# Opening of a gated attention-and-experts layer: first weight loaded by tile, the norm's root ahead of the weight's absolutes, all weight products on GpSimd, second weight's maxima beside the first's

## The chip, the cores and the metric

The kernel runs on one core of one Trainium2 chip. A core has a matrix engine (TensorE, in the profile PE for its products and PEld for its weight loads), a vector engine (VectorE, DVE), a scalar engine (ScalarE, ACT), a general engine (GpSimd, POOL) and a sync engine (SyncE, SP) that here issues most of the loads and stores. Each engine works through its own list of instructions in order, and waits on semaphores for the others. The metric is the device time of one execution in microseconds.

## What is computed

The input is `x`, four batches of 512 tokens with 512 features. Two layers follow, each with a residual. The first is a SmoothQuant pair of int8 linears with a gated unit between them, with the weights `fside` (512 x 512, in the kernel `wi`) and `ctx` (512 x 256, `wc`), one of each per batch. The second is a mixture of sixteen experts, top two per token, beside a shared expert.

```python
def _smooth_quant_linear(x, w):
    amax_x = jnp.max(jnp.abs(x), axis=0)
    amax_w = jnp.max(jnp.abs(w), axis=0)
    s = jnp.sqrt(jnp.maximum(amax_x, EPS) / jnp.maximum(amax_w, EPS))
    xs = x / s
    ws = w * s
    x_scale = jnp.maximum(jnp.max(jnp.abs(xs), axis=-1, keepdims=True), EPS) / QMAX
    w_scale = jnp.maximum(jnp.max(jnp.abs(ws), axis=-1, keepdims=True), EPS) / QMAX
    x_q, w_q = round_and_clip(xs / x_scale), round_and_clip(ws / w_scale)
    return x_q @ w_q.T * x_scale * w_scale.T

x = x + tanh(g_xattn) * down(silu(gate) * up)      # both by _smooth_quant_linear of layernorm(x)
x = x + tanh(g_ffn) * (experts(layernorm(x)) + shared(layernorm(x)))
```

(`round_and_clip` and the last two lines are shortened here.) What matters below is the order that the formula forces on one linear: the column maxima of `|x|` and of `|w|` must both be known before `s` is; `s` before the products `x / s` and `w * s`; these before their row maxima; and the row maxima before anything can be rounded and multiplied.

## The kernel before

A tile is 128 rows. A batch of `x` is four tiles of 128x512, `wi` is four tiles of 128x512, `wc` four of 128x256. Batches go one after the other through both linears; the shared expert's products on TensorE (float32, 128x512) are there to fill TensorE beside them. After all four batches come the sixteen experts, and at the end the results are gathered and added.

Three parts of the code set the order. The stretch from the second half of batch 0 on is laid out by a planner (`Plan`) that knows estimated durations. Before it, for batch 0 and the start of batch 1, the order is written by hand: `opening.at(time, steps)` puts steps on a list, sorted by the time given and then by their place in the text. The times only sort; nothing waits for them. The list is then run once, and so gives each engine its instructions in that order.

The steps that the change touches, with the lines of the kernel before:

- `load_tokens(b)` and `load_weights(b)` (lines 166 to 175) issue the loads of a batch on SP: four tiles of `x`, then `wi` as one transfer of 1 MB, then `wc` as one of 512 KB. Lines 177 to 179 do this for batches 0 and 1, and after them come the two gates (`tg_x_raw`, `tg_f_raw`), the router's weight `gate_sb` and the shared expert's weights. The loads use eight semaphores in turn, so that SP holds the ninth load back until the first has landed, and so on.
- `f0` is the first linear of batch 0. `f0.stats` are mean and variance of a tile (DVE L289, L290). `f0.norm` has three steps: the variance plus epsilon (DVE L272), its root on ACT (L263), and on DVE a reciprocal and a Newton step that end in `r` and `nmr` (L276 to L283). `f0.abs_max` takes `|x|` of a normed tile on ACT (L448) and folds it into the column maximum on DVE (L452).
- `wide0` are the column maxima of `wi`, `narrow0` those of `wc`: `absolute(t)` takes `|w|` of a tile on ACT (L410), `greater(t)` folds it in on DVE (L414), `turn` transposes the maximum on TensorE (L296), `end` reduces it and takes a reciprocal on DVE (L421 to L423). The absolutes of tile 0 have a buffer of their own (`amw`), the others share three (`ab`) with those of `x`.
- `f0.turn_max` and `f0.column_max` do the same for `x` (L296, L464). `f0.smooth` has three steps: the quotient under the root (DVE L313), its root on ACT (L263), and on DVE a Newton step and reciprocals (L318 to L322).
- `f0.row_rs` and `f0.row_s` spread `1/s` and `s` over all partitions (TensorE L304); the second is copied to SBUF by ACT (L475, `s_row`).
- `f0.divide(t)` makes `xn` (DVE L485), `f0.multiply(t)` makes `wi * s` on POOL or DVE (L490). `f0.max_x` and `f0.max_w` are the row maxima, each one reduction over four tiles on DVE (L328), `scale_x` and `scale_w` the small steps behind them (L334 to L339).
- `steps_x`, `steps_w` round to int16 (ACT L348, DVE L346), `turn_x_tile` and `turn_w_tile` transpose on TensorE (L358), `take_x` and `take_w` copy out of PSUM (L351), `product(t)` multiplies (TensorE L565), `scale(t)` writes `h` (DVE L573), and silu, `times_up` and the column maxima of the gated result follow (L576, L583, L587, L590).
- `s0` is the second linear of batch 0, with steps of the same names; its `multiply(t)` is L637, and its `max_w` is again L328.
- `f1.stats(t)`, the statistics of batch 1, are put in between, where they are thought to fit.

PSUM tiles come from three pools: `ps_t` (two buffers), `ps_c` (two) and `ps_mm` (four). `chain_ps` in the code stands for the first two, `beside_ps` for the third.

Of the kernel before, what the change touches and what calls it, by code (L numbers as in the profile page):

```python
# [14 lines left out]
AF = mybir.ActivationFunctionType  # L15
# [105 lines left out]
def flamingo_gated_kernel(  # L121
# [44 lines left out]
    def load_tokens(b):  # L166
        for t in range(TT):
            nc.sync.dma_start(out=X[:, b * TT + t, :], in_=x_flat[:, b * TT + t, :])

    def load_weights(b):  # L170
        wi = qa.tile([P, HC, H], F32, tag="wi", name="wi", bufs=2)
        nc.sync.dma_start(out=wi, in_=w_in[b].rearrange("(t p) d -> p t d", p=P))
        wc = qb.tile([P, HC, A], F32, tag="wc", name="wc", bufs=2)
        nc.sync.dma_start(out=wc, in_=w_ctx[b].rearrange("(t p) d -> p t d", p=P))
        W[b].wi, W[b].wc = wi, wc

    for b in range(2):
# [79 lines left out]
    def small(n, name):  # L257
        return stat.tile([P, n], F32, tag=name, name=name)
# [67 lines left out]
    def row_max(t3, h):  # L326
        sc = small(TT, "sc" + h)
        vec.tensor_reduce(sc, t3, axis=AX.X, op=ALU.max, apply_absolute_value=True)  # L328
        return sc
# [68 lines left out]
    def weights(b, ps=chain_ps):  # L398
        w = W[b]
        w.raw = {}  # L400

        def part(w3, n, h):
            v = SimpleNamespace()

            v.ab = {}
# [6 lines left out]
            def greater(t):  # L412
                v.am = v.ab[0]
                vec.tensor_tensor(v.am[:, :n], v.am[:, :n], v.ab[t][:, :n], ALU.max)  # L414

            def turn():
                v.tp = columns(ps, v.am, n // P)

# [4 lines left out]
                vec.reciprocal(raw, raw)  # L423
                w.raw[n // P] = raw

            return SimpleNamespace(absolute=absolute, greater=greater, turn=turn, end=end)

        return part(lambda: w.wi, H, "i"), part(lambda: w.wc, A, "c")


    def first(b):
# [102 lines left out]
        def sent_w():  # L534
            steps_to_float(w.wqT)

        def max_w():
            w.ws = row_max(w.wi, "w1")

        def scale_w():  # L540
            v.rws = row_scales(w.ws, "w1")
# [63 lines left out]
    def second(b):  # L605
# [75 lines left out]
        def sent_w():  # L681
            steps_to_float(v.wqT)

        def max_w():
            v.ws = row_max(w.wc, "w2")

        def scale_w():
            v.rws = row_scales(v.ws, "w2")
# [563 lines left out]
    opening.at(27.0, *each(f0.steps_x), *each(f0.turn_x_tile))  # L1252
    opening.at(30.0, lambda: f0.steps_w(3), *each(f0.steps_w, vec, ts=[0, 1, 2]))
    opening.at(30.5, *each(f0.turn_w_tile, ts=[0, 1, 3, 2]), lambda: f0.take_x(0, vec), lambda: f0.take_x(2, act))
    opening.at(32.0, lambda: f0.take_w(0, vec), lambda: f0.take_w(2, act), f0.row_ws, *each(narrow0.absolute), *each(narrow0.greater, ts=[1, 2, 3]))
    opening.at(33.6, lambda: f0.product(0), lambda: f0.scaled(0), lambda: f0.product(1), lambda: f0.times_up(0))
    opening.at(35.0, narrow0.turn, lambda: f0.scaled(1), lambda: f0.times_up(1), lambda: f0.gated_abs(0), narrow0.end)
    opening.at(36.0, lambda: f0.product(2), lambda: f0.scaled(2), lambda: f0.times_up(2), lambda: f0.gated_abs(1))
    opening.at(37.0, lambda: f0.product(3), lambda: f0.scaled(3), lambda: f0.gated_greater(1))
    opening.at(38.7, lambda: f0.times_up(3, vec), lambda: f0.gated_max(2), lambda: f0.gated_max(3))  # L1260
# [487 lines left out]
```

## Time and profile before

| what | value |
|---|---|
| median of 3 runs | 585.71 us (585.59 to 585.83) |
| the profiled execution, its own time | 585.57 us |
| its span, first to last instruction | 583.5 us |
| PE busy in the span | 529.3 us, 91% |
| DVE busy | 405.1 us, 69% |
| ACT busy | 228.9 us, 39% |
| POOL busy | 138.2 us, 24% |
| DMA, mean | 163 GB/s |

The span is 2.1 us shorter than the execution's time; these lie outside the first and last instruction. The busy tenths of the page's forty slices (14.6 us each) show where PE isn't full:

```profile
PE   0375499999999999999989999999999999999994
```

Every digit but the first five and the last is 8 or 9. The opening, which the change rewrites, is in these first five slices.

A line of the timeline, as used below, has the start of a group of instructions in us from the span's start, how long the group took, the engine, the line of the kernel, the operation, what it writes and reads, its shape and how many instructions the group has; in brackets stands idle time of the engine before it and what ended it.

### The profile page before, as it was taken

To read this page: it belongs to the slowest core of one execution; us is meant where nothing else is said; L and a number is where in the kernel's file an instruction comes from. 1 tells how busy PE (TensorE), PEld (TensorE's weight loads), DVE (VectorE), ACT (ScalarE), POOL (GpSimd) and SP (SyncE) were. 2 spreads that over 40 slices of the span, in tenths; PEclk is the share of its full clock that TensorE was granted. 3 is DMA by queue.
4 is the path that set the end of the run, shared out by engine and by line. 5 is a ranking of instruction groups with operands and counts; after the bars stand their busy time and mean duration, and the time that the engine had idled before them with its cause. 6 is when DMAs were issued, how large, how long until landed. Compare 5 with 4: busy or idle time off the path is not lost.

```text
span 583.5 us, 5816 instructions
## 1 busy us (share of the span) xinstructions
PE 529.3 (91%) x1760; PEld 275.0 (47%) x1764; DVE 405.1 (69%) x926; ACT 228.9 (39%) x380; POOL 138.2 (24%) x152
## 2 busy tenths in 40 slices
PE   0375499999999999999989999999999999999994
PEld 0232345444444444454455555555555555544441
DVE  3878778998999898987278666666666666304474
ACT  3465366646824272050135434434435343211000
POOL 1212130344143421100310111111212110007770
PEclk9995699999999999999999999999999999999999
DMA  8971012011402365010587999999999995215695
GB/s 295 359 229 38 0 54 92 0 38 54 91 1 54 56 232 155 20 72 1 131 209 223 264 249 269 276 236 276 262 260 274 276 276 173 87 72 160 200 319 187
DMA packets 93774, 95.05 MB, mean 163 GB/s; under 512 B 51488, under 2 KB 69920, under 8 KB 93744
## 3 DMA queue, kind: packets, MB, share of 16 engines
q1 hardware_dynamic: 84016, 69.52, 44.5%
q0 software_dynamic: 5120, 16.78, 9.2%
q10 hardware_dynamic: 4608, 8.39, 3.8%
q8 instruction: 14, 0.23, 0.2%
q14 instruction: 16, 0.13, 0.1%
HBM read 66.36 MB, written 16.78 MB: 142 GB/s over the span
## 4 chain that ended last, share of the span: by engine, by line
PE 79%; DVE 4%; issue 2%; POOL 1%; ACT 0%; DVEq 0%; POOLq 0%
PE b L1138 22%; PE eo L974 14%; PE pu L959 11%; PE pg L959 11%; PE sh L1024 9%; PE pr L998 2%; PE tp_h L1158 2%; PE acc L565 2%; PE sh L1030 1%; PE rowb L304 1%; PE acc L713 1%; DVE amw_w L414 1%; PE tp_am L296 1%; PE tp_x L760 1%; PE tp_q L358 1%
## 5 line engine op out<-in xcount | busy, mean ns | idle before, releaser
L974 PE MATMUL eo<-wd,ehT 128*128 128x512 f32 (+1 forms) x192 | 85.1, 592 | 0.0
L1089 POOL DMA_INDIRECT xg<-xn_dram,slot_token x32 | 34.8, 1088 | 195.7 <-DMA xp<-xg 161.0
L959 PE MATMUL pg<-xT,wsg 128*128 128x512 f32 x160 | 75.7, 603 | 0.0
L959 PE MATMUL pu<-xT,wsu 128*128 128x512 f32 x160 | 74.0, 595 | 0.0
L1024 PE MATMUL sh<-wsd,hT 128*128 128x512 f32 x160 | 73.9, 597 | 0.0
L974 PEld LDWEIGHTS eo<-wd,ehT 128*128 128x128 f32 (+1 forms) x192 | 36.4, 190 | 42.1 <-issue 37.7
L351 ACT COPY xgT<-xp 128x1024 int16<-128x1024 int16 x31 | 39.5, 1339 | 26.4 <-DMA xp<-xg 26.3
L1187 DVE TENSOR_TENSOR p<-p,b 128x352 f32<-128x352 f32 x16 | 8.3, 521 | 58.8 <-PE b L1138 58.8
L1659 POOL DMA_INDIRECT yk<-eo_dram,slot x32 | 33.5, 1048 | 55.7 <-PE pu L959 46.3
L959 PEld LDWEIGHTS pu<-xT,wsu 128*128 128x128 f32 x160 | 29.3, 190 | 31.2 <-issue 31.1
L1024 PEld LDWEIGHTS sh<-wsd,hT 128*128 128x128 f32 x160 | 28.9, 190 | 31.4 <-issue 30.4
L959 PEld LDWEIGHTS pg<-xT,wsg 128*128 128x128 f32 x160 | 29.0, 193 | 30.3 <-issue 29.5
L1138 PE MATMUL b<-T,S 128*128 128x352 f32 x128 | 40.6, 460 | 0.7 <-DVE S L1129 0.7
L1138 PE MATMUL b<-wg,xgT 128*128 128x352 f32 x128 | 40.6, 460 | 0.0
L1138 PE MATMUL b<-wu,S 128*128 128x352 f32 x128 | 40.5, 459 | 0.0
L1149 ACT COPY eo_sb<-eo 128x512 f32<-128x512 f32 x32 | 18.7, 585 | 47.5 <-PE eo L974 43.5
L1138 PEld LDWEIGHTS b<-T,S 128*128 128x128 f32 x128 | 24.2, 190 | 14.5 <-issue 1.2
L1138 PEld LDWEIGHTS b<-wu,S 128*128 128x128 f32 x128 | 24.3, 190 | 13.5
L490 POOL TENSOR_TENSOR wi<-wi,s_row 128x512 f32<-128x512 f32 x15 | 18.6, 1274 | 46.8 <-ACT s_row L475 46.8
L966 DVE TENSOR_TENSOR hT<-g,pu 128x512 f32<-128x512 f32 x20 | 13.6, 682 | 22.6 <-PE pu L959 22.2
L963 ACT ACTIVATE g<-pg 128x512 f32<-128x512 f32 x20 | 11.9, 596 | 41.9 <-PE pg L959 35.6
L1670 DVE SCALAR_TENSOR_TENSOR X<-yk,wk,X 128x512 f32<-128x512 f32 x32 | 23.1, 748 | 7.4 <-DMA yk<-eo_dram,slot 7.1
(219 smaller groups left out, 857.5 us busy)
## 6 DMA issues: line engine op xcount, KB each, us to landing
wg<-in_L_ffn_w_gate_dram SPq DMA_DIRECT2D x16, 704.0 KB, 5.0
wu<-in_L_ffn_w_up_dram SPq DMA_DIRECT2D x16, 704.0 KB, 6.2
wd<-in_L_ffn_w_down_dram SPq DMA_DIRECT2D x16, 512.0 KB, 5.8
eo_dram<-eo_sb ACTq DMA_DIRECT2D x32, 256.0 KB, 4.7
X<-in_x_dram SPq DMA_DIRECT2D x16, 256.0 KB, 8.3
wi<-in_fside_BxS2xS_dram SPq DMA_DIRECT2D x4, 1024.0 KB, 7.1
xn_dram<-yp SPq DMA_DIRECT2D x16, 256.0 KB, 2.0
out_dram<-X SPq DMA_DIRECT2D x16, 256.0 KB, 4.2
```

The lines of the kernel that those rows point to most:

```text
L351: return (vec.tensor_copy if on is vec else act.copy)(dst, src)
L490: on.tensor_tensor(w.wi[:, t, :], w.wi[:, t, :], v.s_row, ALU.mult)
L959: pe.matmul(v.ps[name], lhsT=w[:, k, o : o + P], rhs=xT[:, k, :], start=(k == 0), stop=(k == HC - 1))
L963: act.activation(v.g, v.ps["pg"], AF.Silu)
L966: vec.tensor_tensor(dst, v.g, v.ps["pu"], ALU.mult)
L974: pe.matmul(acc, lhsT=hT[:m, c, bass.ts(t, P)], rhs=wd[:m, c, :], start=(c == 0), stop=(c == len(chunks) - 1))
L1024: pe.matmul(accs[t], lhsT=s.hT[:, c, bass.ts(t, P)], rhs=wsd[:, c, :], start=(c == 0), stop=(c == last))
L1089: pool.indirect_dma_start(out=xg.rearrange("p l n -> p (l n)"), out_offset=None, in_=xn_dram, in_offset=bass.IndirectOffsetOnAxis(ap=slot_ ...
L1138: pe.matmul(ps[:, :I], lhsT=lhs[:, k, :], rhs=rhs[:, k, :], start=(first and k == 0), stop=(k == HALF - 1), skip_group_check=not first,)
L1149: act.copy(eo, R[e].acc[h])
L1659: pool.indirect_dma_start(out=yk, out_offset=None, in_=eo_dram, in_offset=bass.IndirectOffsetOnAxis(ap=slot[i % 2][:, tiles[i // 2] : tile ...
L1670: vec.scalar_tensor_tensor(X[:, j, :], yks[added[0]], wk[k][:, j : j + 1], X[:, j, :], ALU.mult, ALU.add)
```

## The change

It rewrites the loads ahead of the opening and the list of the opening, and splits three helpers.

Loads: `wi` of batch 0 is four transfers of 256 KB, one a tile, in place of one of 1 MB; the two gates and `gate_sb` are issued right behind `wc` of batch 0, ahead of the loads of batch 1.

```diff
     def load_weights(b):
         wi = qa.tile([P, HC, H], F32, tag="wi", name="wi", bufs=2)
-        nc.sync.dma_start(out=wi, in_=w_in[b].rearrange("(t p) d -> p t d", p=P))
+        wi_src = w_in[b].rearrange("(t p) d -> p t d", p=P)
+        for ts in [slice(t, t + 1) for t in range(HC)] if b == 0 else [slice(0, HC)]:
+            nc.sync.dma_start(out=wi[:, ts, :], in_=wi_src[:, ts, :])
...
-    for b in range(2):
-        load_tokens(b)
-        load_weights(b)
+    load_tokens(0)
+    load_weights(0)
...
     nc.sync.dma_start(out=gate_sb[:E], in_=gate_w)
+    load_tokens(1)
+    load_weights(1)
```

Helpers: `greater_both(t)` folds a tile into the maximum without an absolute on ACT, by two instructions on DVE that read the raw weight. `narrow` of batch 0 takes its PSUM tile from `beside_ps`. `max_w` of either linear may be called for some of the tiles.

```diff
+            def greater_both(t):
+
+                v.am, raw = v.ab[0], w3()[:, t, :]
+                vec.scalar_tensor_tensor(v.am[:, :n], raw, -1.0, v.am[:, :n], ALU.mult, ALU.max)
+                vec.tensor_tensor(v.am[:, :n], v.am[:, :n], raw, ALU.max)
...
-        return part(lambda: w.wi, H, "i"), part(lambda: w.wc, A, "c")
+        return part(lambda: w.wi, H, "i", ps), part(lambda: w.wc, A, "c", beside_ps if b == 0 else ps)
...
-        def max_w():
-            w.ws = row_max(w.wi, "w1")
+        def max_w(ts=slice(0, HC)):
+            if ts.start == 0:
+                w.ws = small(HC, "scw1")
+            vec.tensor_reduce(w.ws[:, ts], w.wi[:, ts, :], axis=AX.X, op=ALU.max, apply_absolute_value=True)
```

The list of the opening, up to the second linear's quantized weight:

```diff
-    opening.at(8.4, *f0.norm, every=0.3)
-    opening.at(8.4, *each(wide0.absolute, ts=[0, 1]))
-    opening.at(10.3, lambda: wide0.greater(1), *each(f0.abs_max), *each(wide0.absolute, ts=[2, 3]))
-    opening.at(13.2, *each(wide0.greater, ts=[2, 3]))
-    opening.at(14.2, f0.turn_max, wide0.turn, f0.column_max, lambda: f1.stats(0), wide0.end)
-    opening.at(18.0, *f0.smooth[:2])
-    opening.at(18.5, f0.smooth[2], f0.row_rs, f0.row_s, gates)
-    opening.at(19.5, lambda: f1.stats(1), lambda: table(AF.Silu), gate_columns)
-    opening.at(20.7, *each(f0.divide), *each(f0.multiply, ts=[0, 1, 2]), f0.max_x, f0.scale_x)
-    opening.at(26.5, lambda: f0.multiply(3, vec), f0.max_w, f0.scale_w, f0.open_turns)
+    opening.at(7.7, *f0.norm[:2])
+    opening.at(8.0, lambda: wide0.absolute(0), f0.norm[2], lambda: wide0.greater_both(1))
+    opening.at(9.2, *each(f0.abs_max), f0.turn_max, *each(wide0.absolute, ts=[2, 3]))
+    opening.at(12.8, *each(wide0.greater, ts=[2, 3]), wide0.turn, f0.column_max)
+    opening.at(15.2, *each(narrow0.absolute, ts=[1, 2]), wide0.end, f0.smooth[0], lambda: narrow0.absolute(0), *f0.smooth[1:])
+    opening.at(17.8, f0.row_rs, f0.row_s, lambda: narrow0.absolute(3), lambda: narrow0.greater(1), lambda: f1.stats(0))
+    opening.at(18.5, gates, lambda: table(AF.Silu), gate_columns)
+    opening.at(19.0, *each(f0.divide), *each(f0.multiply), f0.max_x, f0.scale_x)
+    opening.at(22.5, lambda: f0.max_w(slice(0, HC - 1)), lambda: f0.max_w(slice(HC - 1, HC)), f0.scale_w, f0.open_turns)
...
-    opening.at(32.0, lambda: f0.take_w(0, vec), lambda: f0.take_w(2, act), f0.row_ws, *each(narrow0.absolute), *each(narrow0.greater, ts=[1, 2, 3]))
-    opening.at(33.6, lambda: f0.product(0), lambda: f0.scaled(0), lambda: f0.product(1), lambda: f0.times_up(0))
+    opening.at(28.0, lambda: f0.take_w(0, vec), lambda: f0.take_w(2, act), f0.row_ws, *each(narrow0.greater, ts=[2, 3]))
+    opening.at(29.6, lambda: f0.product(0), lambda: f1.stats(1), lambda: f0.scaled(0), lambda: f0.product(1), lambda: f0.times_up(0))
...
-    opening.at(43.7, s0.divide, lambda: s0.multiply(0), lambda: s0.multiply(1), s0.max_a, s0.scale_a)
-    opening.at(46.6, lambda: s0.multiply(2, vec), lambda: s0.multiply(3, vec), s0.max_w, s0.scale_w, s0.open_turns)
+    opening.at(43.7, s0.divide, *each(s0.multiply), s0.max_a, s0.scale_a)
+    opening.at(46.6, lambda: s0.max_w(slice(0, HC - 1)), lambda: s0.max_w(slice(HC - 1, HC)), s0.scale_w, s0.open_turns)
```

The lines left out between these differ in their times alone, and nothing moves by that. By engine, before against after: on ACT the root of the norm moves ahead of the first absolute of `wi`, the absolute of `wi` tile 1 is gone, and the four absolutes of `wc` move from behind `ws_row` to around the root of `s` (tiles 1, 2, 0 ahead of it, tile 3 behind `s_row`). On DVE two instructions of `greater_both` replace one fold, the statistics of batch 1 move (tile 0 behind the Newton step of `s`, tile 1 behind two folds of `wc`), one fold of `wc` moves behind that Newton step, three products (one 128x512, two 128x256) are gone, and each of two reductions becomes two. POOL has four products in place of three in the first linear, and four in place of two in the second. TensorE's list, and every list behind the opening, keeps its order.

More of the change, by code (lines that the diff above doesn't have):

```diff
@@ L400, in weights, with part @@
         w.raw = {}
-        def part(w3, n, h):
+        def part(w3, n, h, ps):
             v = SimpleNamespace()
@@ L424, in end @@
                 w.raw[n // P] = raw
-            return SimpleNamespace(absolute=absolute, greater=greater, turn=turn, end=end)
-        return part(lambda: w.wi, H, "i"), part(lambda: w.wc, A, "c")
+            return SimpleNamespace(absolute=absolute, greater=greater, greater_both=greater_both, turn=turn, end=end)
+        return part(lambda: w.wi, H, "i", ps), part(lambda: w.wc, A, "c", beside_ps if b == 0 else ps)
     def first(b):
@@ L682, in sent_w, with max_w @@
             steps_to_float(v.wqT)
-        def max_w():
-            v.ws = row_max(w.wc, "w2")
+        def max_w(ts=slice(0, HC)):
+            if ts.start == 0:
+                v.ws = small(HC, "scw2")
+            vec.tensor_reduce(v.ws[:, ts], w.wc[:, ts, :], axis=AX.X, op=ALU.max, apply_absolute_value=True)
         def scale_w():
@@ L1250, in flamingo_gated_kernel @@
-    opening.at(20.7, *each(f0.divide), *each(f0.multiply, ts=[0, 1, 2]), f0.max_x, f0.scale_x)
-    opening.at(26.5, lambda: f0.multiply(3, vec), f0.max_w, f0.scale_w, f0.open_turns)
-    opening.at(27.0, *each(f0.steps_x), *each(f0.turn_x_tile))
-    opening.at(30.0, lambda: f0.steps_w(3), *each(f0.steps_w, vec, ts=[0, 1, 2]))
-    opening.at(30.5, *each(f0.turn_w_tile, ts=[0, 1, 3, 2]), lambda: f0.take_x(0, vec), lambda: f0.take_x(2, act))
-    opening.at(32.0, lambda: f0.take_w(0, vec), lambda: f0.take_w(2, act), f0.row_ws, *each(narrow0.absolute), *each(narrow0.greater, ts=[1, 2, 3]))
@@ L1256, in flamingo_gated_kernel @@
-    opening.at(33.6, lambda: f0.product(0), lambda: f0.scaled(0), lambda: f0.product(1), lambda: f0.times_up(0))
[L1257 to L1260, printed above, removed]
+    opening.at(7.7, *f0.norm[:2])
@@ new lines, in flamingo_gated_kernel @@
+    opening.at(18.5, gates, lambda: table(AF.Silu), gate_columns)
+    opening.at(19.0, *each(f0.divide), *each(f0.multiply), f0.max_x, f0.scale_x)
+    opening.at(22.5, lambda: f0.max_w(slice(0, HC - 1)), lambda: f0.max_w(slice(HC - 1, HC)), f0.scale_w, f0.open_turns)
+    opening.at(23.0, *each(f0.steps_x), *each(f0.turn_x_tile))
+    opening.at(26.0, lambda: f0.steps_w(3), *each(f0.steps_w, vec, ts=[0, 1, 2]))
+    opening.at(26.5, *each(f0.turn_w_tile, ts=[0, 1, 3, 2]), lambda: f0.take_x(0, vec), lambda: f0.take_x(2, act))
@@ new lines, in flamingo_gated_kernel @@
+    opening.at(28.0, lambda: f0.take_w(0, vec), lambda: f0.take_w(2, act), f0.row_ws, *each(narrow0.greater, ts=[2, 3]))
+    opening.at(29.6, lambda: f0.product(0), lambda: f1.stats(1), lambda: f0.scaled(0), lambda: f0.product(1), lambda: f0.times_up(0))
+    opening.at(31.0, narrow0.turn, lambda: f0.scaled(1), lambda: f0.times_up(1), lambda: f0.gated_abs(0), narrow0.end)
+    opening.at(32.0, lambda: f0.product(2), lambda: f0.scaled(2), lambda: f0.times_up(2), lambda: f0.gated_abs(1))
+    opening.at(33.0, lambda: f0.product(3), lambda: f0.scaled(3), lambda: f0.gated_greater(1))
@@ L1261, in flamingo_gated_kernel @@
+    opening.at(34.7, lambda: f0.times_up(3, vec), lambda: f0.gated_max(2), lambda: f0.gated_max(3))
     opening.at(40.0, lambda: table(AF.Sqrt), s0.turn_max, lambda: f1.stats(2), s0.column_max, *s0.smooth)
     opening.at(43.0, s0.row_rs, s0.row_s, lambda: f1.stats(3))
-    opening.at(43.7, s0.divide, lambda: s0.multiply(0), lambda: s0.multiply(1), s0.max_a, s0.scale_a)
-    opening.at(46.6, lambda: s0.multiply(2, vec), lambda: s0.multiply(3, vec), s0.max_w, s0.scale_w, s0.open_turns)
+    opening.at(43.7, s0.divide, *each(s0.multiply), s0.max_a, s0.scale_a)
```

## Prediction

> **What bounds it.** First the busy times by stretch, then the waits of the stretch that isn't full. The columns are busy us and instructions of PE, PEld, DVE, ACT and POOL, the clock, the DMA share and GB/s.
>
> ```profile
> 0.00:66.00 66.00, 23.31 (x106) 13.05 (x109) 49.37 (x117) 29.32 (x54) 14.65 (x30) 0.87 0.62 204
> ...
> 79.00:290.00 211.00, 209.96 (x741) 98.81 (x742) 176.35 (x482) 94.03 (x160) 60.16 (x63) 1.00 0.25 70
> ```
>
> ```profile
> PE tp_x L760 <- DVE y L740: 7.3, 1, 7.3
> ```
>
> From 79 us on TensorE is full. Before 66.0 us it works a third of the time, and its last wait there, 7.3 us, is for the normed tiles `y` at the end of batch 0's two linears. So the opening is one chain of dependent steps, TensorE's full stretch hangs on its end, and a microsecond off the chain is one off the total. The change keeps every list behind the opening in order, so a gain isn't given back by another order there.
>
> The chain is in the timeline, and I read who was late at each join:
>
> ```profile
> 8.08 0.17 DVE L272 TENSOR_SCALAR ve<-mv 128x4 f32<-128x4 f32 x1
> 10.24 0.55 SPq L183 DMA_DIRECT2D tg_x_raw<-in_g_xattn_dram  x1
> 10.25 0.63 ACT L410 ACTIVATE amw_w<-wi 128x512 f32<-128x512 f32 x1 [7.96 <-DMA wi<-in_fside_BxS2xS_dram]
> ...
> 11.31 0.19 ACT L263 ACTIVATE r<-ve 128x4 f32<-128x4 f32 x1
> ...
> 12.53 0.81 ACT L448 ACTIVATE amx<-X,nmr,r 128x512 f32<-128x512 f32 x1 [1.03 <-DVE nmr L283]
> ...
> 20.41 0.20 ACT L263 ACTIVATE s<-s 128x4 f32<-128x4 f32 x1 [3.91 <-DVE s L313]
> ...
> 24.36 3.72 POOL L490 TENSOR_TENSOR wi<-wi,s_row 128x512 f32<-128x512 f32 x3 [20.93 <-ACT s_row L475]
> ...
> 28.63 0.69 DVE L490 TENSOR_TENSOR wi<-wi,s_row 128x512 f32<-128x512 f32 x1
> 28.75 2.56 ACT L348 ACTIVATE xq<-xn,rscx 128x512 int16<-128x512 f32 x4 [1.26 <-DVE rscx L339]
> 29.43 2.29 DVE L328 TENSOR_REDUCE scw<-wi 128x4 f32<-128x2048 f32 x1
> ...
> 32.16 1.28 DVE L346 TENSOR_SCALAR wq<-wi,rscw 128x512 int16<-128x512 f32 x3
> ...
> 38.62 1.40 DVE L573 SCALAR_TENSOR_TENSOR h<-acc,scx,ws_row 128x512 f32<-128x512 f32 x2
> ```
>
> The root `r` has its input at 8.25 and runs at 11.31, behind two absolutes that wait for `wi` until 10.25. That is the first 3 us. All later joins are late by what DVE has to do.
>
> **Part 1: loads, norm's root, `greater_both`.** The root now leads: ACT 8.29 to 8.49, then the same 0.96 us of DVE steps as from 11.53 to 12.49, so `nmr` at 9.48. The absolute of tile 0 (0.63) must fit in between. When does tile 0 of `wi` land? The four `x` tiles land at 3.6, 4.2, 5.7 and 7.1 (their readers' starts), `wi` as a whole at 10.2: 3.1 us for 1 MB, 0.78 a tile. With four transfers in the same queue I take 7.9, 8.7, 9.5, 10.2. [...] Ends: tile 0 at 7.8, or with the last at 10.2.
>
> So ACT has the absolute at 8.52 to 9.15 and `amx` at 9.52 in place of 12.53: **-3.0**. `greater_both` is 0.74 (like L573, a scalar_tensor_tensor of this size) plus 0.69 (L452) from 9.5 to 11.0, while DVE would wait for ACT until 11.06: nothing, and 0.7 late if that cover were gone. The other absolutes of `wi` come at 12.35, behind all landings. Batch 1's tile statistics no longer stand ahead of `rawi` (19.10, TensorE was ready at 18.97): -0.1. Sum at `s`: **-3.1**, root at 17.3. On ACT three absolutes of `wc` (0.42 each) now stand ahead of it; `wc` landed at 11.7 and the last of them needs the PSUM transposes of `wi`, at 15.9, so ACT is free at 16.4. Behind the Newton step a fold of `wc` (0.42) and one statistics pair (0.87) give DVE at 19.75, against 19.7 for TensorE's row of `1/s`: nothing. The gates' loads move ahead on SP by six loads, so they land near 12 and the tables (3.2 us of ACT after `s_row`) end at 24.8, before ACT is next needed. On SP three more issues at 0.43 put `wc` at 4.5 in place of 3.1, with `x` still queued. Of eight loads in flight, the gates and `gate_sb` now wait for `x` tiles (4.2 to 7.1), batch 1's tiles for those of `wi` (from 7.9, with over 1 MB still queued in front of them: no gap). Their first reader is at 18.9; behind them stand `wi` and `wc` of batch 1 and the shared expert's weights, read from 66 us on.
>
> **Part 2: all `wi` products on POOL.** DVE loses 0.69 and the reduction is cut (1.75 + 0.69 against 2.29, from the slope between 128x1024, 1.22, and 128x2048): alone that is -0.5. But POOL is now busy from 21.2 to 26.2 (4.95), and DVE ends `max_x` at 24.8 in the middle of it. What happens to small DVE steps there is shown by batch 2, where POOL has all four products:
>
> ```profile
> 142.68 1.12 DVE L334 TENSOR_TENSOR scx<-scx,r 128x4 f32<-128x4 f32 x1
> 143.83 1.19 DVE L335 TENSOR_SCALAR scx<-scx 128x4 f32<-128x4 f32 x1
> ```
>
> A 128x4 step takes 1.12 and 1.19 us in place of 0.17. POOL's third and fourth products there end at 143.78 and 145.00 (L490, 1.27 each), 0.02 before these two do: each waits for a whole POOL product. The same phase holds here, `scale_x` meeting the third product 3.6 us after POOL's start, so L334 waits to 24.95, L335 to 26.2, and L337, L339 end at 26.6. Before, with POOL done at 28.08, they ended at 28.71. So the rounding of `x` gains only 2.1, and the reductions run 26.5 to 28.9, `scale_w` to 29.35, `wq` at 29.4 against 32.16: **-2.75**. Part 2 costs 0.35 net. Without this wait it would be 28.4, -3.8.
>
> **Part 3: `wc` folds out of the way.** Before, `h` starts at 38.62, behind three folds of `wc`; its product ended near 37.6. Now two folds and one statistics pair (1.8 us) lie between `take_w` (32.4) and 34.2, and the product ends at 34.8, so `h` starts there: 1.0 more. The second `h` waits for its own product (35.7), the last two for DVE, then the third and fourth product: `h` ends at 38.65 against 42.16, and the fold of the gated maxima keeps its 2.1 us behind it. **-3.5**. `narrow.turn` has its own PSUM pool and waits for nothing.
>
> **Part 4: `wc` products on POOL.** DVE loses 0.75, the cut reduction is 0.95 + 0.42 for 1.22, and L335 of `scale_a` waits 0.25 for POOL's third product (rows of 0.28 in batches 1 and 2 stand for this). `cq` comes 0.5 sooner, TensorE is held by the transposes of `aq` behind that wait. I take **-0.45**; ends 0 and -0.6.
>
> **Sum.** -3.0 -0.1 +0.35 -0.75 -0.45 = -3.95. On the profiled execution's 585.57 that is 581.6; the median shown is 0.14 above it, so I predict **581.6**.
>
> **Rivals.**
> - *The waits on POOL miss* (0.15). If the phase differs or small steps slip between products, `wq` is at 28.4, and nearly all of the 1.0 survives: -5.0, 580.6. For: L334 in the present run lost only 0.02. Against: batch 2, the same four products.
> - *The head start is halved* (0.19). If tile 0 lands with the whole at 10.2, `amx` is at 10.9, 1.4 less: 583.0. Or TensorE's slow pace lasts longer: the first six of L565 take 2.38 us, 0.4 each, the last eight 1.89, 0.24 each; should the last eight go at 0.4 too, that is 1.3 to 1.7 more: 583.2. For: the pace changes at a moment that the change moves. Against: TensorE is busier just ahead of it than before.
> [...]
> - *It doesn't reach the end* (0.05): TensorE's full stretch takes up the head start because a load or the clock fixes its pace: 585.5. Loads for it have landed by 40 us and are read after 66, which speaks against.
>
> **Numbers.** Forecast 0.55, and its own range is 580.8 to 582.4 (the ends of Part 4, 0.3 for Part 1, 0.3 for Part 3). The range over the first three cases is 580.3 to 583.4. Differences under 0.2% (1.2 us) can't be told from none here. Faster by more than that: 0.55 + 0.15 + 0.19 = 0.89; same 0.05; slower 0.06.
>
> **What would show it.** `amx` near 9.5 and the first `wi` landing near 8; L334 and L335 of the first linear at over 0.1 and over 1 us, ending with POOL's third and fourth products; `wq` at 29.4, `h` at 34.9, `cq` near 49.0, and the first `tp_x` at 62.0 in place of 66.0, with the rest of the kernel as long as before. I am wrong if the gap at `tp_x` is not the gap in the total, or if `wc` lands after 16 us.

## The result, and the profile after

The changed kernel takes **579.45 us** (median of 5 runs, 578.75 to 579.89) beside 585.69 us for the kernel before on the same chip (5 runs, 584.87 to 585.83): ratio 0.9899, 95% interval 0.9889 to 0.991. That is 6.2 us faster. The forecast was 581.6, 4.0 us faster, with a range that began at 580.3: the direction was right, the gain came out half as large again, and the time lies outside the range.

The profiled execution took 579.45 us, its span 577.3 (before: 585.57 and 583.5), so 6.12 us less. First the waits of the first 66 us (engine, line, what it waited for: us in total, times, longest), then the busy times by stretch, with the columns of the prediction:

```profile
PE tp_x L773 <- DVE y L753: 7.5, 1, 7.5
```

```profile
0.00:60.16 60.16, 21.95 (x106) 12.83 (x108) 50.08 (x117) 29.03 (x53) 17.21 (x33) 0.85 0.66 223
73.15:284.15 211.00, 210.12 (x742) 98.94 (x742) 176.41 (x482) 94.04 (x160) 60.14 (x63) 1.00 0.25 70
```

The wait at `tp_x` is still there and hardly longer (7.3 before); it ends at 60.16 instead of 66.00. A full stretch of 211 us behind it has 210.1 us of TensorE work, where the same stretch had 210.0 before. So the opening is shorter, and the rest runs almost as it did. The chain in the timeline after (start, us, engine, line, operation, out<-in; in brackets the idle time before it and what ended it; the code has moved down by some lines, so L335 of the prediction is L338 here):

```profile
7.32 0.17 DVE L275 TENSOR_SCALAR ve<-mv 128x4 f32<-128x4 f32 x1
7.52 0.20 ACT L266 ACTIVATE r<-ve 128x4 f32<-128x4 f32 x1 [5.23 <-DVE ve L275]
7.63 0.61 ACT L413 ACTIVATE amw_w<-wi 128x512 f32<-128x512 f32 x1
...
8.76 0.81 ACT L457 ACTIVATE amx<-X,nmr,r 128x512 f32<-128x512 f32 x1 [0.51 <-DVE nmr L286]
...
16.54 0.21 ACT L266 ACTIVATE s<-s 128x4 f32<-128x4 f32 x1 [0.92 <-DVE s L316]
...
20.50 4.93 POOL L499 TENSOR_TENSOR wi<-wi,s_row 128x512 f32<-128x512 f32 x4 [17.07 <-ACT s_row L484]
...
24.06 0.18 DVE L337 TENSOR_TENSOR scx<-scx,r 128x4 f32<-128x4 f32 x1
24.27 1.19 DVE L338 TENSOR_SCALAR scx<-scx 128x4 f32<-128x4 f32 x1
...
28.59 1.28 DVE L349 TENSOR_SCALAR wq<-wi,rscw 128x512 int16<-128x512 f32 x3
...
31.67 1.96 PE L576 MATMUL acc<-wqT,xqT 128*128 128x512 bf16 x7
...
33.27 1.39 DVE L584 SCALAR_TENSOR_TENSOR h<-acc,scx,ws_row 128x512 f32<-128x512 f32 x2
...
35.39 1.41 DVE L584 SCALAR_TENSOR_TENSOR h<-acc,scx,ws_row 128x512 f32<-128x512 f32 x2
...
47.18 1.14 DVE L349 TENSOR_SCALAR cq<-wc,rscw 128x256 int16<-128x256 f32 x4
```

The same places in both traces, with what the prediction said of them (us; the last column is what the step alone gave, the difference between one shift and the one above it):

| place | before | after | shift | forecast of the shift | step alone: measured (forecast) |
|---|---|---|---|---|---|
| `amx` starts | 12.53 | 8.76 | -3.77 | -3.0 | -3.77 (-3.0) |
| root of `s` | 20.41 | 16.54 | -3.87 | -3.1 | -0.10 (-0.1) |
| `wq` starts | 32.16 | 28.59 | -3.57 | -2.75 | +0.30 (+0.35) |
| last `h` ends | 42.16 | 36.80 | -5.36 | -3.5 | -1.79 (-0.75) |
| `cq` starts | 53.02 | 47.18 | -5.84 | -3.95 | -0.48 (-0.45) |
| first `tp_x` | 66.00 | 60.16 | -5.84 | -3.95 | 0 (0) |
| whole execution | 585.57 | 579.45 | -6.12 | -3.95 | -0.28 (0) |

In three of the seven rows the step alone differs from the forecast by more than 0.1: in the first by 0.77, in the fourth by 1.04, in the last by 0.28. The experiments are about the first two.

In the first row the input of the root came early: `ve` stands at 7.32 here and at 8.08 before, because the last of the four `x` tiles landed at 6.35 us instead of 7.11. From `ve` to `amx` it takes 1.44 us; the prediction had 9.52 less 8.08, which is 1.44 too. In the fourth row TensorE does the first seven products in 1.96 us, all but the first 0.22 apart. Before, most of them were 0.43 apart, and `h` stood behind the folds of `wc` besides:

```profile
36.09 2.38 PE L565 MATMUL acc<-wqT,xqT 128*128 128x512 bf16 x6 [0.22 <-issue]
36.79 0.96 DVE L414 TENSOR_TENSOR amw_w<-amw_w,ab_w 128x256 f32<-128x256 f32 x2 [1.68 <-ACT ab_w L410]
38.27 0.42 DVE L414 TENSOR_TENSOR amw_w<-amw_w,ab_w 128x256 f32<-128x256 f32 x1 [0.53 <-DVE amw_w L414]
```

### The profile page after: what moved, and what is told of

Its sections match the earlier page's. It is cut to its first block, busy times and chain, and to the rows that moved or that the text cites. A ratio compares the mean times of both kernels' runs of the same rounds, so it can differ in the third digit from the quotient of the medians.

```text
span 577.3 us, 5824 instructions
## 1 busy us (share of the span) xinstructions
PE 527.8 (91%) x1760; PEld 274.8 (48%) x1764; DVE 405.7 (70%) x926; ACT 228.7 (40%) x379; POOL 140.3 (24%) x155
## 4 chain that ended last, share of the span: by engine, by line
PE 83%; DVE 4%; DMA 1%; issue 0%; ACT 0%; DVEq 0%; SPq 0%
PE b L1151 22%; PE eo L987 14%; PE pu L972 12%; PE pg L972 11%; PE sh L1037 11%; PE pr L1011 2%; PE tp_h L1171 2%; PE acc L576 2%; PE sh L1043 1%; PE rowb L307 1%; DMA wg<-in_L_ffn_w_gate_dram 1%; PE acc L726 1%; DVE amw_w L417 1%; PE tp_x L773 1%; PE tp_am L299 1%; PE tp_q L361 1%
## 5 line engine op out<-in xcount | busy, mean ns | idle before, releaser
L499 POOL TENSOR_TENSOR wi<-wi,s_row 128x512 f32<-128x512 f32 x16 | 19.8, 1274 | 43.0 <-ACT s_row L484 43.0
L979 DVE TENSOR_TENSOR hT<-g,pu 128x512 f32<-128x512 f32 x20 | 13.7, 683 | 22.8 <-PE pu L972 22.2
L1151 PEld LDWEIGHTS b<-wg,xgT 128*128 128x128 f32 x128 | 23.1, 190 | 10.9 <-issue 0.8
```

The lines of the kernel that those rows point to most:

```text
L499: on.tensor_tensor(w.wi[:, t, :], w.wi[:, t, :], v.s_row, ALU.mult)
L979: vec.tensor_tensor(dst, v.g, v.ps["pu"], ALU.mult)
L1151: pe.matmul(ps[:, :I], lhsT=lhs[:, k, :], rhs=rhs[:, k, :], start=(first and k == 0), stop=(k == HALF - 1), skip_group_check=not first,)
```

## The experiments

Two theories for each surplus. For the landing: **S**, four transfers for the first weight make the `x` tile ahead of them land sooner, so the change did it; or **scatter**, it lands anywhere within some range in every execution, and the profile of before happened to show a late one. For the products: the change keeps TensorE busier and so fast (**cause**), or the pace at that moment is again a draw of each execution, and what the change did is to make it count (**draw**). In the texts below theory O is that the order of the loads moved the landing, and C is scatter.

### One part at a time

**The split alone**, on the kernel before:

```diff
-        nc.sync.dma_start(out=wi, in_=w_in[b].rearrange("(t p) d -> p t d", p=P))
+        wi_src = w_in[b].rearrange("(t p) d -> p t d", p=P)
+        for ts in [slice(t, t + 1) for t in range(HC)] if b == 0 else [slice(0, HC)]:
+            nc.sync.dma_start(out=wi[:, ts, :], in_=wi_src[:, ts, :])
```

> The kernel before with one edit: wi of batch 0 in four transfers, its loads' order and the opening's list untouched. ACT still has both absolutes ahead of the root, but they can start with the first and second tile. Theory S (the split lets the last x tile land sooner, at 6.4 in place of 7.1): wi tiles land near 7.3 and 8.0, the first absolute of x starts near 9.6 in place of 12.5, total 585.7 - 2.9 = 582.8. Theory O (the order of the loads did it) and theory C (it was that one execution's chance): x at 7.1, wi tiles near 7.9 and 8.7, the absolute of x near 10.4, total 583.6.

Measured: 581.76 us (6 runs, 580.96 to 582.22), ratio 0.9935 (0.9922 to 0.9949). Its timeline:

```profile
7.11 0.63 ACT L412 ACTIVATE amw_w<-wi 128x512 f32<-128x512 f32 x1 [4.82 <-DMA wi<-in_fside_BxS2xS_dram]
7.33 0.17 DVE L274 TENSOR_SCALAR ve<-mv 128x4 f32<-128x4 f32 x1
...
8.27 0.19 ACT L265 ACTIVATE r<-ve 128x4 f32<-128x4 f32 x1
...
9.49 0.81 ACT L450 ACTIVATE amx<-X,nmr,r 128x512 f32<-128x512 f32 x1 [1.03 <-DVE nmr L285]
```

The first tile of `wi` lets ACT go at 7.11 where it stood until 10.25, so the split alone brings `amx` 3.04 us ahead and is worth 3.9 of the 6.2 us. That is 1.0 more than the most that was expected; 0.43 of it is that `h` ends 9.57 us behind `wq` here and 10.00 before (see the folds, below), and the rest is not explained. The root still stands behind two absolutes: with `ve` at 7.33 it runs at 8.27, and in the changed kernel, with `ve` at 7.32, at 7.52. So moving the root, with `greater_both`, is worth another 0.73 at `amx` (9.49 to 8.76).

**The order of the loads alone**, on the kernel before:

```diff
-    for b in range(2):
-        load_tokens(b)
-        load_weights(b)
+    load_tokens(0)
+    load_weights(0)
...
     nc.sync.dma_start(out=gate_sb[:E], in_=gate_w)
+    load_tokens(1)
+    load_weights(1)
```

> The kernel before with the other edit of the loads: gates and router weight ahead of batch 1's loads, wi still one transfer. S: nothing moves, last x tile at 7.1, wi at 10.2, first absolute of x at 12.5, total 585.7. O: the last x tile at 6.4, wi near 9.4, the absolute of x near 11.7, total 584.9. C: somewhere between, with no system over the runs.

Measured: 585.28 us (13 runs), ratio 0.9998 (0.9988 to 1.0007). The order gives nothing that shows (the interval is 0.7 us to either side at most). `amx` starts at 12.16, 2.30 us behind the landing of the whole `wi` at 9.86, and the last `x` tile lands at 6.59, between the two values that S and O named.

**The changed kernel without the split:**

```diff
-        for ts in [slice(t, t + 1) for t in range(HC)] if b == 0 else [slice(0, HC)]:
+        for ts in [slice(0, HC)]:
```

> The changed kernel with wi of batch 0 in one transfer again. S: last x tile at 7.1, wi at 10.2, absolute of x at 10.9 in place of 8.8, total 579.45 + 2.1 = 581.6. O: x at 6.4, wi at 9.4, absolute of x at 10.0, total 580.7.

Measured: 581.34 us (6 runs, 580.1 to 581.66), ratio 0.9923 (0.9908 to 0.9938), so 1.9 us slower than with the split. Its timeline:

```profile
8.84 0.20 ACT L266 ACTIVATE r<-ve 128x4 f32<-128x4 f32 x1 [6.55 <-DVE ve L275]
11.01 0.63 ACT L413 ACTIVATE amw_w<-wi 128x512 f32<-128x512 f32 x1 [1.97 <-DMA wi<-in_fside_BxS2xS_dram]
11.55 0.80 ACT L457 ACTIVATE amx<-X,nmr,r 128x512 f32<-128x512 f32 x1
```

The root is early, but the absolute of tile 0 stands ahead of `amx` on ACT and waits for the whole weight: `amx` is at 11.55, 0.56 us behind the landing of `wi` at 10.99, where it was 2.30 behind it before. So without the split the new order ahead of `amx` is worth 1.74 us there, with it only 0.73; the split is worth 3.04 by itself. The two don't add up: together they give 3.77 and not 4.78. (Both landings of this profile, `x` at 7.67 and `wi` at 10.99, are the latest of all profiles.)

**The fourth product of `wi` back on VectorE**, on the changed kernel:

```diff
-    opening.at(19.0, *each(f0.divide), *each(f0.multiply), f0.max_x, f0.scale_x)
-    opening.at(22.5, lambda: f0.max_w(slice(0, HC - 1)), lambda: f0.max_w(slice(HC - 1, HC)), f0.scale_w, f0.open_turns)
+    opening.at(19.0, *each(f0.divide), *each(f0.multiply, ts=[0, 1, 2]), f0.max_x, f0.scale_x)
+    opening.at(22.5, lambda: f0.multiply(3, vec), f0.max_w, f0.scale_w, f0.open_turns)
```

> The changed kernel with the fourth wi product of the first linear back on DVE and one reduction over all four tiles. Theory L (the small steps of scale_x wait for whole products of POOL, 1.0 us in the changed kernel): the wait of the scaling step goes, 1.19 becomes 0.17, the rounding of x starts at 25.1 in place of 25.9, DVE has 0.69 more behind it, wq near 28.2 in place of 28.6, total 579.45 - 0.4 = 579.0. Rival N (what DVE executes counts, the wait is not on the chain): wq 0.5 later, total 580.0.

Measured: 579.38 us (5 runs, 578.76 to 580.93), ratio 0.9898 (0.9881 to 0.9915): the same as the changed kernel. The profiled execution is the longest of the five, 580.93. Its timeline:

```profile
24.45 0.17 DVE L338 TENSOR_SCALAR scx<-scx 128x4 f32<-128x4 f32 x1
...
28.47 1.28 DVE L349 TENSOR_SCALAR wq<-wi,rscw 128x512 int16<-128x512 f32 x3
...
32.41 2.56 PE L576 MATMUL acc<-wqT,xqT 128*128 128x512 bf16 x6 [0.22 <-issue]
33.57 0.75 DVE L584 SCALAR_TENSOR_TENSOR h<-acc,scx,ws_row 128x512 f32<-128x512 f32 x1 [0.34 <-PE acc L576]
35.01 0.75 DVE L584 SCALAR_TENSOR_TENSOR h<-acc,scx,ws_row 128x512 f32<-128x512 f32 x1 [0.68 <-PE acc L576]
...
36.41 1.41 DVE L584 SCALAR_TENSOR_TENSOR h<-acc,scx,ws_row 128x512 f32<-128x512 f32 x2
```

L338 takes 0.17 us again: the 1.19 was a wait for GpSimd's fourth product. Counted from `ve` (7.50 here), `wq` starts after 20.97 us in place of 21.27, 0.30 sooner, which is the price that the forecast put on Part 2 (0.35). But in this execution TensorE does the products 0.43 apart, VectorE now waits for them (0.34 and 0.68), and `h` ends 9.34 us behind the start of `wq` in place of 8.21. The edit takes no work from TensorE ahead of the products, so this is the first sign that the pace is a draw. The time itself, between the two that were expected (579.0 and 580.0), can't tell a gain of 0.3 from none.

### The folds, and TensorE's pace

The next four kernels ran on a chip on which the kernel before took 595.24 us, and in all four profiles TensorE stands still for some us in the last part of the shared expert. Here is that row for the changed kernel with fillers (see below; behind the bar stand busy us, mean ns and the idle time before it); in the changed kernel's own profile, from another chip, its idle time is 0.0:

```profile
L1037 PE MATMUL sh<-wsd,hT 128*128 128x512 f32 x160 | 75.7, 608 | 8.0 <-issue 8.0
```

That standstill is 7.3 to 12.2 us in the four profiles and swamps a microsecond in the opening. In three of the four TensorE waits there for VectorE's `hT` (L979); what holds that up stays open, since on this chip the kernel before was run without a profile and the changed kernel not at all. So these four are read by their traces up to the first `tp_x`, and their ratios tell little.

**The folds of `wc` back where they stood**, on the changed kernel:

```diff
-    opening.at(15.2, *each(narrow0.absolute, ts=[1, 2]), wide0.end, f0.smooth[0], lambda: narrow0.absolute(0), *f0.smooth[1:])
-    opening.at(17.8, f0.row_rs, f0.row_s, lambda: narrow0.absolute(3), lambda: narrow0.greater(1), lambda: f1.stats(0))
+    opening.at(15.2, wide0.end, *f0.smooth)
+    opening.at(17.8, f0.row_rs, f0.row_s, lambda: f1.stats(0), lambda: f1.stats(1))
...
-    opening.at(28.0, lambda: f0.take_w(0, vec), lambda: f0.take_w(2, act), f0.row_ws, *each(narrow0.greater, ts=[2, 3]))
+    opening.at(28.0, lambda: f0.take_w(0, vec), lambda: f0.take_w(2, act), f0.row_ws, *each(narrow0.absolute), *each(narrow0.greater, ts=[1, 2, 3]))
```

> The changed kernel with the second weight's absolutes and folds back where they stood before the change (behind the maxima of the scales of w, ahead of `h`), and batch 1's second statistics ahead of the divisions. Theory (these folds on VectorE delay the head of `h` whatever TensorE's pace): `h` begins about 6.0 us after wq as in the split alone (6.03) instead of 4.68, and ends 9.57 after wq instead of 8.21, so 1.36 later: 580.8. Rival, the prediction's own size for this part: 0.75 later, 580.2. Rival (TensorE's pace is all of it, the folds nothing): the same as the changed kernel if the pitch is 0.22.

Measured: 590.76 us, ratio 0.9928 (0.9902 to 0.9955). Its timeline:

```profile
31.98 1.51 PE L576 MATMUL acc<-wqT,xqT 128*128 128x512 bf16 x6 [0.15 <-ACT wqT L354]
...
33.06 0.42 DVE L417 TENSOR_TENSOR amw_w<-amw_w,ab_w 128x256 f32<-128x256 f32 x1 [1.67 <-ACT ab_w L413]
34.02 0.96 DVE L417 TENSOR_TENSOR amw_w<-amw_w,ab_w 128x256 f32<-128x256 f32 x2 [0.54 <-ACT ab_w L413]
34.90 1.41 DVE L584 SCALAR_TENSOR_TENSOR h<-acc,scx,ws_row 128x512 f32<-128x512 f32 x2
...
37.04 1.41 DVE L584 SCALAR_TENSOR_TENSOR h<-acc,scx,ws_row 128x512 f32<-128x512 f32 x2
```

The products are done by 33.5, at the quick pace, and `h` still starts only at 34.90, behind folds that wait 1.67 us for ACT's absolutes. It ends 10.01 us behind `wq` (28.44 to 38.45), 1.80 later than in the changed kernel; 1.36 was expected. The rest is the gap of 0.54 between two folds. Of the five profiles with the folds ahead of `h` four have it (0.53 or 0.54), and the split alone has not; what ends it stays open.

**The products of `wc` back on two engines**, on the changed kernel:

```diff
-    opening.at(43.7, s0.divide, *each(s0.multiply), s0.max_a, s0.scale_a)
-    opening.at(46.6, lambda: s0.max_w(slice(0, HC - 1)), lambda: s0.max_w(slice(HC - 1, HC)), s0.scale_w, s0.open_turns)
+    opening.at(43.7, s0.divide, lambda: s0.multiply(0), lambda: s0.multiply(1), s0.max_a, s0.scale_a)
+    opening.at(46.6, lambda: s0.multiply(2, vec), lambda: s0.multiply(3, vec), s0.max_w, s0.scale_w, s0.open_turns)
```

> The changed kernel with the second weight's products as before the change (two on GpSimd, two on VectorE, one maximum). The prediction's sum for its Part 4: `cq` begins 11.2 us instead of 10.4 us after `h` ends (before 10.86, after 10.38), so 0.45 to 0.48 later, and the end with it: 579.9. Rival (something else ends last there): the same, 579.4.

Measured: 589.59 us, ratio 0.9901 (0.9874 to 0.9927). In its trace `cq` starts 10.86 us behind the end of `h` (37.53 to 48.39), in the changed kernel 10.38: 0.48, the difference that was expected (the 11.2 in the expectation doesn't fit its own 0.48). `tp_x` keeps it (12.96 us behind `cq`, 12.98 there). The other profiles with these products on GpSimd and no later fillers have 10.29 to 10.38, those with two engines 10.85 to 10.94.

**TensorE kept busy:** products of two constants, whose result nobody reads, ahead of its first turns.

```diff
+    def fill(n):
+        def step():
+            d = beside_ps[0]([P, H], F32, "fill")
+            for _ in range(n):
+                pe.matmul(d[:, :P], lhsT=ident, rhs=ones, start=True, stop=True)
+        return step
...
+    opening.at(3.0, fill(34))
...
-    opening.at(12.8, *each(wide0.greater, ts=[2, 3]), wide0.turn, f0.column_max)
+    opening.at(12.8, *each(wide0.greater, ts=[2, 3]), wide0.turn, f0.column_max, fill(7))
...
-    opening.at(18.5, gates, lambda: table(AF.Silu), gate_columns)
+    opening.at(18.5, gates, lambda: table(AF.Silu), gate_columns, fill(20))
```

> The changed kernel with matmuls on two constants put between TensorE's early work (34 ahead of the absolute maxima's turns, 7 after the last fold's turn, 20 ahead of the first turns of x), so that TensorE is hardly idle before the first products. Pace theory (TensorE's slow pace at the first products is what moved the head of `h` by 1 us between the kernels): the pitch of the first products is 0.22 us in the trace and the clock's record is fast well ahead of 31 us; `h` begins by 33.3 as in the changed kernel's profile, the turns ahead of it may save 0.3 us; time 579.0, the spread of the five runs under 0.8. Rival (the pace has nothing to do with TensorE's idle time before it): the pitch is 0.43 in this or in some other run, spread as before, 579.4. Rival (fillers stand in the way of real turns): the root of `s` later than 16.6 by 0.3 or more, 579.8 to 580.5.

Measured: 588.75 us (587.07 to 590.18), ratio 0.9886 (0.9858 to 0.9914). Its timeline on TensorE:

```profile
13.11 0.66 PE L299 MATMUL tp_am<-ident,amx 128*128 128x128 f32 x4 [1.12 <-DVE amx L461]
14.51 0.66 PE L299 MATMUL tp_am<-ident,amw_w 128*128 128x128 f32 x4 [0.74 <-DVE amw_w L417]
```

Each of these turns takes 1.09 and 1.12 us in the changed kernel, where TensorE comes to them from idleness. The rows of `1/s` go from 1.11 to 0.65. `wq` starts 20.16 us behind `ve` in place of 21.27: 1.1 us of the opening was TensorE's slow pace at small turns, which the forecast had not looked at, as both kernels have it alike. The clock's record, which in the changed kernel begins with a turn to full at 31.80, is at full from 7.03 to 27.51 here. Then it is at half until 30.92, just ahead of the first product at 30.97. So the pitch of 0.22 and the early `h` came, but not a clock that is full well ahead of them, and the runs spread over 3.1 us where under 0.8 was expected.

**The same with the fourth product of `wi` on VectorE:**

> As the one before, and the fourth product of the first weight back on VectorE with one maximum over all of wi, as in the kernel before the change. If the pace alone had hidden that edit's worth: VectorE's L338 no longer waits (0.1 us where it took 1.19), xq begins 0.84 us sooner than in the changed kernel, at 25.0, wq 0.1 to 0.3 sooner at 28.3 to 28.5, the first products run at 0.22, `h` begins at 33.0 and the end is 0.3 sooner than that of the fillers alone: 578.8. If the wait is not what wq waits for: wq unchanged at 28.6, the same time as the fillers alone.

Measured: 593.38 us, ratio 0.9958 (0.9935 to 0.998), with the longest of the standstills, 12.2 us. `wq` starts 20.46 us behind `ve`, 0.3 later than with the fillers alone, where 0.1 to 0.3 sooner was expected: a miss. Half of the 0.3 lies ahead of the root of `s`, where the edit changes nothing (`amx` to `s` 7.48 and 7.33); from there to `wq` it is 11.54 and 11.39, so the edit costs 0.15. In the profile of the fillers alone the wait for GpSimd has become shorter:

```profile
19.62 4.97 POOL L499 TENSOR_TENSOR wi<-wi,s_row 128x512 f32<-128x512 f32 x4 [16.18 <-ACT s_row L484]
23.87 0.74 DVE L337 TENSOR_TENSOR scx<-scx,r 128x4 f32<-128x4 f32 x1
24.64 0.17 DVE L338 TENSOR_SCALAR scx<-scx 128x4 f32<-128x4 f32 x1
```

VectorE comes to its small steps later in GpSimd's fourth product: L337 takes 0.74 us until that product ends and L338 no longer waits, so 0.56 us of waiting is left of 1.0, less than the product costs VectorE (0.69).

### Both kernels once more

> The kernel before once more, for a second profile. Theory S: the last x tile lands at 7.1 or later. Rival (scatter): at 6.0 to 6.7 as in the kernels with four transfers. The first products run at 0.43 or at 0.22; `h` begins 6.0 to 6.5 us after wq either way, because VectorE's folds set it.

> The changed kernel once more, for the same chip as the next two, and for a second look at where its opening stands. Theory S (a first weight in four transfers lets the last x tile land sooner): that tile lands at 6.0 to 6.7 us again. Rival (its landing scatters by as much, whatever the transfers): 7.0 or later. Either way wq begins 21.1 to 21.4 us after the variance `ve` (21.27 in the first profile, 21.27 in the one with the second weight's products on VectorE). The ratio to the kernel before: 0.989 to 0.991.

Measured on one chip: 585.23 us before (7 runs), 579.61 after (4 runs, 579.3 to 580.31), ratio 0.9907 (0.9891 to 0.9924). The second profile of the kernel before settles the landing:

```profile
5.92 0.66 DVE L289 BATCH_NORM_STATS2 bn<-X 128x6 f32<-128x512 f32 x1
...
6.83 0.17 DVE L272 TENSOR_SCALAR ve<-mv 128x4 f32<-128x4 f32 x1
...
10.52 0.63 ACT L410 ACTIVATE amw_w<-wi 128x512 f32<-128x512 f32 x1 [8.23 <-DMA wi<-in_fside_BxS2xS_dram]
...
11.57 0.19 ACT L263 ACTIVATE r<-ve 128x4 f32<-128x4 f32 x1
...
12.79 0.81 ACT L448 ACTIVATE amx<-X,nmr,r 128x512 f32<-128x512 f32 x1 [1.03 <-DVE nmr L283]
```

Here, with one transfer for the weight, the last `x` tile lands at 5.63, 1.5 us sooner than in the first profile, and `ve` is at 6.83. `amx` doesn't notice: it is 2.29 us behind the landing of `wi` (10.50), as in the first profile (2.30 behind 10.23). The changed kernel's second profile has the landing at 6.67, which S had named too and which by itself decides nothing. But S needed 7.1 or later here. **S falls.** Over ten profiles with four transfers the last `x` tile lands from 5.88 to 7.24 us, 6.52 in the mean; over four with one transfer from 5.63 to 7.67, 6.75 in the mean. An effect of the size of that difference, 0.2 us, can't be told from none.

The pace is read by laying the profiles without fillers side by side, the kernels whose folds stand ahead of `h` first. The clock's record switches between half and full in stretches of 3.41 us and its multiples (6.83, 13.65, 3.41 and 10.24 us in the first profiles of both kernels, from 37.95 and 31.80 on); the third column is when it turned to full around the first products:

| kernel | first product | full clock from | turned, us behind the first product | `h` ends, us behind `wq` |
|---|---|---|---|---|
| before | 35.24 | 37.95 | 2.7 | 10.00 |
| before, again | 35.51 | 37.33 | 1.8 | 10.00 |
| order of the loads alone | 34.87 | 36.03 | 1.2 | 9.99 |
| split alone | 32.20 | 32.76 | 0.6 | 9.57 |
| after, folds late | 31.45 | 31.34 | -0.1 | 10.01 |
| after, one transfer | 34.23 | 33.20 | -1.0 | 7.99 |
| after | 31.67 | 31.80 | 0.1 | 8.21 |
| after, again | 31.98 | 32.89 | 0.9 | 8.27 |
| after, `wc` on VectorE | 31.93 | 33.66 | 1.7 | 8.67 |
| after, fourth `wi` on VectorE | 31.55 | 34.64 | 3.1 | 9.34 |

In the first five rows, with the folds ahead of `h`, the pace makes no difference: four end alike with turns 2.8 us apart, and the fifth lacks the gap between the folds. In the last five, without the folds, a later turn goes with a later `h`, over 1.35 us. And the moment of the turn lies anywhere within 4.1 us; between two profiles of one kernel it differs by 0.9 and 0.8. **Draw** stands for most of it. A small effect of the change is not excluded: the turn lies 1.6 us behind the first product in the mean of rows 1 to 4, where the list of the opening is as before the change, and 0.8 in the mean of the six others.

### More fillers

The first fillers (34, 7, 20) and 53 more in TensorE's later gaps of the opening:

```diff
-    opening.at(33.0, lambda: f0.product(3), lambda: f0.scaled(3), lambda: f0.gated_greater(1))
+    opening.at(33.0, lambda: f0.product(3), lambda: f0.scaled(3), lambda: f0.gated_greater(1), fill(11))
-    opening.at(40.0, lambda: table(AF.Sqrt), s0.turn_max, lambda: f1.stats(2), s0.column_max, *s0.smooth)
-    opening.at(43.0, s0.row_rs, s0.row_s, lambda: f1.stats(3))
+    opening.at(40.0, lambda: table(AF.Sqrt), s0.turn_max, lambda: f1.stats(2), s0.column_max, fill(7), *s0.smooth)
+    opening.at(43.0, s0.row_rs, s0.row_s, fill(13), lambda: f1.stats(3))
...
-    opening.at(53.5, lambda: s0.product(2), lambda: s0.residual(1), lambda: s0.stats(0), lambda: s0.product(3))
+    opening.at(53.5, lambda: s0.product(2), lambda: s0.residual(1), lambda: s0.stats(0), lambda: s0.product(3), fill(22))
```

> The changed kernel with the fillers of the run before (34, 7 and 20 ahead of the first turns of x) and more of them in TensorE's later gaps: 11 after the last product of `h`, 7 and 13 around the second statistics, 22 ahead of the first tp_x. Pace theory: TensorE at its fast pace through the opening: besides the 1.1 us of the first fillers, the four turns of the absolute maxima (0.60 to 0.35), the rows (0.69 to 0.40), the eight turns of aq, the first product of the second linear and the 16 turns of y (3.76 to some 2.0) take 2 us less on the chain: tp_x ends and `pg` begins 3 us sooner after `ve` than in the changed kernel (57.28 there), at 54.3; the end 3 us sooner than the same chip's run of the changed kernel, ratio to before 0.984. Rival (VectorE and ScalarE set that stretch, TensorE's pace shows only in tp_x): 1.1 + 1.5, ratio 0.986. Rival (fillers hold real turns up): no better than the first fillers, 0.988.

Measured: **577.75 us** (4 runs, 577.28 to 578.06), ratio 0.9873 (0.9857 to 0.989), on the chip where the changed kernel took 579.30 to 580.31. This version beats both, by 7.5 and 1.9 us, where 3 was expected. `pg` starts 54.9 us behind `ve`, in the changed kernel 57.3 and 56.9, so 2.0 to 2.4 us of the 3 are there. Part of the head start is lost again 160 us later, at a row where the changed kernel's wait is 0.12 and 0.14 us:

```profile
222.18 0.62 PE L307 MATMUL rowb<-ident,scw 128*128 128x128 f32 x4 [1.36 <-DVE scw L338]
```

At 215 us this profile is 3.3 us ahead of the changed kernel's second one (0.6 of it from an earlier `x`), at the end 2.1. TensorE has come so far ahead that VectorE is late with a scale of batch 1, which looks like the next bound; no run tested it.

**With the fourth product of `wi` on VectorE as well:**

> As the one before, with the fourth product of the first weight on VectorE and one maximum. In the profiles so far wq begins 20.16 us after `ve` with the first fillers, 20.46 with the first fillers and this edit, so on this chain the edit costs 0.3 at fast pace: the end 0.3 later than the run before. Rival (from the first run of this edit, 21.27 to 20.97 at slow pace): 0.3 sooner.

Measured: 579.54 us (4 runs, 578.49 to 580.19), ratio 0.9896 (0.988 to 0.9913), 1.8 later than the fillers alone, where 0.3 was expected: a miss. In its profile the products run 0.43 apart although fillers stand ahead of them (the clock turned to half at 27.69 and to full at 34.52), and `h` ends 9.27 us behind `wq` in place of 7.96; the last `x` tile lands at 7.24 in place of 5.88. So the profiled execution, the longest of the four, met both draws at their late end, and the edit itself is 0.15 of it (`wq` 20.30 us behind `ve`, 20.15 without). Why the other three runs are slower too (578.49 at the least, against 578.06 at the most with the fillers alone) no trace shows. With fillers the clock turned to full 1.2 us ahead of the first product to 2.9 behind it (four profiles), without them 1.0 ahead to 3.1 behind: they speed up the small turns, but that they make the pace at the products quick is not shown.

## Why the prediction was too small

**What held.** The opening is one chain, and what leaves the chain leaves the total: 5.84 us at `tp_x`, 6.12 in all. Tile by tile the first weight landed at 7.29, 7.96, 8.63 and 9.33, so 0.67 to 0.70 us apart, where 7.9 to 10.2 was taken. For the chance of 0.06 that the change makes the kernel slower the runs show no ground: `wc` landed at 10.92 us, and ACT stood idle for 0.92 us just ahead of the root of `s`. `greater_both` and the moved absolutes cost nothing on the chain (`s` 0.10 sooner than `amx`, as forecast). The wait for GpSimd in Part 2 came as named: L338 takes 1.19 us and ends at 25.46, with GpSimd's four products (20.50 and 4.93), and the experiment without it returns 0.30. Part 4 gave 0.48 for 0.45. One claim was wrong without harm: the loads do have a gap. From 10 to 11 us they move 62 GB/s where it was 379 before, and the second batch's weight lands at 17.79 instead of 17.15, long before anyone reads it.

**What failed, 1: Part 1's term of -3.0 rests on `x` landing at 7.1, read off one profile.** It should have been -3.8 in this execution and some -3.6 in the mean: the landing scatters from 5.6 to 7.7, and 7.11 was a late draw. In the kernel before nobody can see it, since `wi` lands 3 us later and sets `amx`. Once the root leads and the weight comes by tile, `ve` comes 1.0 to 1.1 us behind the landing and `amx` 1.44 behind `ve`. Size: 0.76.

**What failed, 2: Part 3's term of -0.75 keeps TensorE's slow pace for the first products.** It had `h` end 9.25 us behind `wq` (29.4 to 38.65), and it is 8.21. At the slow pace the part is worth 0.66 (10.00 to 9.34); at the pace of the changed kernel's profile 1.79. The pace was for the most part a draw as well, and hidden as well, under the folds of `wc`. The rival that named the pace had it only as a risk in the slow direction. The stretches of 3.41 us in the clock's record and the scatter of its turns in the table above are what the term left out: two profiles of one kernel lie 0.9 and 0.8 us apart, and the ten profiles of the table span 4.1 us. What sets the moment of a turn no run shows. With the ends measured here, Part 3 would have been a range from -0.7 to -2.0 and, with its middle, the forecast 0.6 lower (an estimate). Size: 1.04.

**What failed, 3:** 0.28 us came behind the opening, where nothing was forecast. Of it, 0.16 arises between 218 and 264 us (from one group of the shared expert's products to the next it is 45.65 us in place of 45.81). There the kernel before waits for VectorE at the row that the fillers later made worse:

```profile
230.35 0.62 PE L304 MATMUL rowb<-ident,scw 128*128 128x128 f32 x4 [0.28 <-DVE scw L335]
```

The changed kernel's wait is 0.12. But the second profile of the kernel before has 0.08 there, and over the twelve profiles without the later fillers it lies from 0.0 to 0.59, so this looks like one more draw and not like the change's work. The second pair of profiles still has 0.20 behind `tp_x` (6.40 in the span, 6.20 at `tp_x`); what makes it stays open, and no experiment was made on it.

Together: 3.95 + 0.76 + 1.04 + 0.28 is 6.03, and the small differences of Parts 1, 2 and 4 (0.01, 0.05 and 0.03) make up the measured 6.12. The range failed for the same reason as the time: it took 0.3 for Part 1 and 0.3 for Part 3, though each hung on a value seen once. The sum explains the two profiled executions, and in that of the changed kernel both draws lay on the early side. With the means of the profiles instead (`x` at 6.52, `h` ending 8.50 us behind `wq` in the last five rows of the table) the same sum gives a gain of some 5.3 us, an estimate; the two pairs of medians measured 6.2 and 5.6.

## What to carry to other kernels

A time that is covered by something later in the chain is one draw when it is read off a trace: before a change takes the cover away, ask how far it scatters, from a second profile or from its siblings in the same one (the four `x` tiles landed 0.6 to 1.4 us apart), and put that spread into the sum, in both directions. When an engine whose clock turned to full at another moment in every profile becomes the one that others wait for, its pace is a range, not a row. And two edits that shorten the same wait (the split and the root's place, 3.04 and 1.74 us at `amx` each by itself) don't add up: together they gave 3.77.

## What was not expected of the hardware

- The last of four queued tiles of 256 KB lands anywhere from 5.6 to 7.7 us, in 14 profiles of nearly the same loads, while the weight behind it, in one transfer, is complete at 9.9 to 11.0.
- Small turns on TensorE cost by what came before them: four of 128x128 took 1.09 us after idleness and 0.66 after fillers. 61 fillers brought `wq` forward by 1.1 us, and 114 of them the whole kernel by 1.9.
